# A two-layer attention and experts kernel on one Trainium2 core: the half-resolution level summed from the projected map, and two experts' first layers run inside the last image

## The chip, the cores and the metric

The kernel runs on one core of one Trainium2 chip. The core has a matrix engine (TensorE, PE in the profile; its weight loads are listed as PEld), a vector engine (VectorE, DVE), a scalar engine (ScalarE, ACT), GpSimd (POOL) and SyncE (SP), which issues most transfers. The metric is the device time of one execution in microseconds (us); the median of several runs is quoted.

## What is computed

The input is eight images of 256 channels and 32 x 32 positions, in fp32. Layer 0 is an attention with eight heads whose keys and values come from four resolutions of the projected image:

```python
kv = jnp.einsum('bchw,oc->bohw', x, kv_w)
k_map, v_map = (kv[:, :C], kv[:, C:])
def pooled(t):
    for i, r in enumerate([1, 2, 3, 6]):
        oh, ow = (round(H / r), round(W / r))       # 32, 16, 11, 5
        p = jnp.einsum('bchw,ph,qw->bcpq', t, Mh, Mw)   # averages
        p = p + _depthwise(p, dconv_w[i], dconv_b[i])   # 3 x 3
...
attn = softmax(q_g @ k * SCALE);  out_att = attn @ v
```

So there are 1024 + 256 + 121 + 25 = 1426 keys an image. Averaging and projection are both linear, so they may be done in either order. Layer 1 is a single-head attention over the 1024 tokens of an image, followed by eight experts of three 256 x 256 products each with a batch norm and a relu after the first two, weighted by a gate that is a softmax over the mean of all images:

```python
h = relu(_bn(jnp.einsum('bfd,edh->bfeh', x, W1) + b1, ...))
h = relu(_bn(jnp.einsum('bfeh,ehk->bfek', h, W2) + b2, ...))
y = jnp.einsum('bfeh,ehd->bfed', h, Wo) + bo
return jnp.einsum('bfed,fe->bfd', y, w)
```

## The kernel before

**Order of the work.** All engines' instructions are written out by a planner, the class `Flow` (lines 657 to 910), which keeps a model of each engine's clock with a price for every instruction (`cost`, line 723; GpSimd's sums are 0.15 + 0.0023 us an element, line 744). The main loop (line 1911) goes through steps: image, half of the heads, half of the queries, chunk of 128 keys. Each step issues four score products, one exponential on ACT over 2048 columns (`scores`, line 1512) and the values of the step before. Two steps' exponentials are added up by a DMA that GpSimd issues (`add`, line 1567), and `sums` (line 1574) adds the pairs on DVE. Between these, the planner resumes generator threads in the order of their rank when PE has room: a step grants 4 us of PE time to ranks below 5 and 2 us to ranks from 5 on (`PACE`, `PACE1`, lines 31 and 32, used in line 1952), and a thread may also run while PE would otherwise wait for the exponential. `finish` runs threads without that limit until something is there that the loop needs.

**Keys and values of the next image.** While image b is attended, the thread `prepare` (rank 4, line 1381) makes image b+1 ready. It normalises the image `xi`, and `pool_levels` (line 1332) makes the 16 x 16, 11 x 11 and 5 x 5 levels of it in `xl`: for each of the two channel halves, GpSimd sums neighbours in a row (`t2`, 512 elements), then neighbouring rows (`l2`, 256 elements) and multiplies by 0.25; then it makes the 11 x 11 level, and DVE the last. `maps` (line 1114) projects four maps m, two of values and two of keys, in three slices of `KEY_SLICES` (line 45): 512, 512 and 402 columns, the last being all three small levels. ACT copies each slice from PSUM into `p` and writes the centre tap of the 3 x 3 filter with its bias into `acc`. The other eight taps are DVE instructions on `p` and `acc` (`taps`, line 1245), run level after level by `convolve` (rank 7). Image 0 has its own versions, `first_maps` (line 1173) and `first_taps` (line 1259). In the narrow form (line 677) a product with 128 output rows is issued as four products of 32 rows that run side by side; the trace records two matmuls for each fp32 product.

**Layer 1 and the experts.** `layer1` (rank 6), `outputs` and `norm` (rank 5) run layer 1 of earlier images between the steps. `ended` counts the images whose normalised result `hn` is in DRAM. After the last image, attention's tiles are given up, and `experts` (line 2095) loads all weights and works on 16 tiles of 512 tokens, tile i from image i (first half) for i below 8; unit i is tile i / 8, expert i % 8. Until the gate is known it runs first and second layers ahead (`ahead`, line 2362) and puts the results into DRAM, `h2d`; after that the loop of line 2445 runs second, third and first layers in turn. The first three first layers, and all second layers before the gate, are plain: four products of 512 columns, eight records. The others take seven products of 256 columns, 14 records, with sums on DVE and GpSimd around them (`products`, line 2252).

Of the kernel before, what the change touches and what calls it, by code (L numbers as in the profile page):

```python
# [26 lines left out]
NE = 8  # L27
# [16 lines left out]
KEY_CHUNKS = [(i * P, min(P, NK - i * P)) for i in range(NKC)]  # L44
KEY_SLICES = [(0, 512), (512, 512), (1024, 402)]


# [864 lines left out]

def attention(tc, kit, f, outer, ended, nb, consts, x, t1, t2, hn, bounds, vecs, q_t, kv_t, proj_t, gqk_t, wqk, wqkv, vecs1, w1_d, w1c, gate_d, wrc, vecs2, bnvec):

# [5 lines left out]
    with ExitStack() as ctx:  # L920
# [16 lines left out]
        def load_x(b):  # L937
            xi = T(work, [P, 2, HW], "xi")
            for k in range(2):
                f.sp.dma_start(xi[:, k, :], x[b, k * P : (k + 1) * P, :])  # L940
            return xi
# [29 lines left out]
        def db(c, s):  # L971
# [5 lines left out]
            mid, vec[:, V_DW : V_DW + 72].rearrange("p (a t) -> p a t", t=9)[:, :, 4], 1.0, None, ALU.add  # L977
        )
        hi, lo = bounds
        for t in bounds:  # L980
# [129 lines left out]
        def source(xp, s0, w):  # L1110
            xi, xl = xp
            return xi[:, :, s0 : s0 + w] if s0 < HW else xl[:, :, s0 - HW : s0 - HW + w]

        def maps(xp):

            for m in (2, 3, 0, 1):
                c = m % 2
                yield until(
                    lambda: read[0] >= len(todo) - 1 and len(todo) < (3 + 2 * max(freed[0], 2) if freed[0] else 5)
                )  # L1120
                p = pmaps[len(todo) % 2]
                acc = T(work, [P, NK], "acc", bufs=3)
                for s0, w in KEY_SLICES:
                    if s0 >= HW:
                        yield until(lambda: len(done) >= len(todo) - 1)
                    src = source(xp, s0, w)
                    yield pe(src, tag="sm")
                    ps = small()
                    for k in range(2):
                        f.pe.matmul(  # L1130
                            ps[:, :w],
                            lhsT=kvw[:, k, m * P : (m + 1) * P],
                            rhs=src[:, k, :],
                            start=k == 0,
                            stop=k == 1,
                        )
                    f.act.activation(p[:, s0 : s0 + w], ps[:, :w], AF.Copy)
                    for s, n in enumerate(SIDES):
                        a, z = max(OFFS[s], s0), min(OFFS[s] + n * n, s0 + w)
                        if a < z:  # L1140
                            f.act.activation(
                                acc[:, a:z],
                                ps[:, a - s0 : z - s0],
                                AF.Identity,
                                bias=db(c, s),
                                scale=mid[:, c * 4 + s : c * 4 + s + 1],
                            )
# [7 lines left out]

        pmaps = [T(work, [P, NK], f"p{i}") for i in range(2)]
        for t in pmaps:
            f.split(t, 512, HW)
        first, large, whole, pooled, asked = {}, [], [], [], []

# [12 lines left out]
        def first_maps(xp):  # L1173
# [13 lines left out]
            for m, s0 in [(m, s0) for g in (0, 2) for s0 in (0, 512) for m in (g, g + 1)] + [(m, HW) for m in range(4)]:  # L1187
                if s0 == HW:
                    yield until(lambda: pooled)
                w = min(512, NK - s0)  # L1190
                c = m % 2
# [4 lines left out]
                for k in range(2):  # L1196
# [6 lines left out]
                    )  # L1203
                small_levels = s0 == HW and m < 2
                f.act.activation(ptail[:, m, :w] if small_levels else p[:, s0 : s0 + w], ps[:, :w], AF.Copy)
                for s, n in enumerate(SIDES):
                    a, z = max(OFFS[s], s0), min(OFFS[s] + n * n, s0 + w)
                    if a < z and (m >= 2 or s):
# [5 lines left out]
                            scale=mid[:, c * 4 + s : c * 4 + s + 1],  # L1214
                        )
                if (m, s0) == (3, 512):
                    large.append("maps")
                    f.spawn(first_keys(0), 1)
                    f.spawn(first_keys(1), 5)
# [39 lines left out]
        def first_taps():  # L1259
# [6 lines left out]
            for m in (0, 1, 2, 3):  # L1266
                p, acc = first[m]
                for s in range(1, 4):
                    yield from taps(m % 2, s, *((ptail[:, m, :], acc, HW) if m < 2 else (p, acc)))
                whole.append(m)  # L1270
            done.extend(first[m][1] for m in (2, 3, 0, 1))

        def convolve():

            for m in range(4, 4 * nb):
                yield until(lambda: len(todo) > m)
                c, p, acc = todo[m]
                for s in range(4):
                    yield from taps(c, s, p, acc)
                    read[0] += s == 0  # L1280
# [51 lines left out]
        def pool_levels(xi, xl):  # L1332
# [3 lines left out]
            def level(s):  # L1336
                n = SIDES[s]
                return xl[:, :, OFFS[s] - HW : OFFS[s] - HW + n * n].rearrange("p k (h w) -> p k h w", h=n)

            for k in range(2):  # L1340
                one, l2, l3 = img[:, k], level(1)[:, k], level(2)[:, k]

                yield pool(xi)
                t2 = T(work, [P, 32, 16], "pool")
                f.pool.tensor_tensor(t2, one[:, :, 0::2], one[:, :, 1::2], ALU.add)
                yield pool(t2)
                f.pool.tensor_tensor(l2, t2[:, 0::2, :], t2[:, 1::2, :], ALU.add)
                yield pool(t2)
                f.pool.tensor_scalar(l2, l2, 0.25, 1.0, ALU.mult, ALU.mult)

# [11 lines left out]
                f.pool.tensor_tensor(l3[:, 1:11, :], l3[:, 1:11, :], t3[:, 2::3, :], ALU.add)  # L1362
                flat = xl[:, k, OFFS[2] - HW : OFFS[3] - HW]
                f.pool.tensor_tensor(flat, flat, con[:, K_S11 : K_S11 + 121], ALU.mult)
# [8 lines left out]
            for i, (a, e) in enumerate(ends):  # L1373
                f.ve.tensor_reduce(
                    l5[:, :, i, :], t5[:, :, a:e, :].rearrange("p k h w -> p k w h"), AX.X, ALU.add
                )
            flat = xl[:, :, OFFS[3] - HW :]
            f.ve.tensor_tensor(flat, flat, con[:, None, K_S5 : K_S5 + 25].to_broadcast([P, 2, 25]), ALU.mult)
            pooled.append(True)

        def prepare(b):
# [28 lines left out]
            for k in range(2):  # L1410
# [3 lines left out]
                )  # L1414
            xl = T(work, [P, 2, NK - HW], "xl")
            if b == 0:
# [59 lines left out]
        def key_tokens(b, g):  # L1476
# [3 lines left out]
            accs = done[4 * b + 2 : 4 * b + 4] if b else [first[m][1] for m in (0, 1)]  # L1480
            kt = T(work, [P, 4, C], "kt")
            yield from by_tokens(accs, kt, 4 * g)
# [397 lines left out]
        mt = T(wp, [P, 2, C], "mt")  # L1880
        bias = T(wp, [P, 2], "mtb")
        def unit(b, c, sl, n, pairs):
            total = yield from sums(n, pairs)
# [12 lines left out]
        f.spawn(chain(mix(), weights1(), outputs()), 5)  # L1896
        f.spawn(layer1(), 6)
        f.columns = True
        order = [*range(8), NKC - 1, *range(8, NKC - 1)]
# [53 lines left out]
        f.columns = False  # L1953
        f.finish(lambda: projected[0] == nb)
        f.also.clear()
        f.finish(lambda: f.free("sx") < NEVER)
# [137 lines left out]

def experts(tc, kit, nb, t2, hn, h2d, w1c, w2_d, wo_d, bnvec, bo_d, gate_d, wrc, consts8, gtd, out, f, outer, ended, early):

# [11 lines left out]
    with ExitStack() as ctx:  # L2108
# [13 lines left out]

        w1, w2, wo = ([T(wp, [P, 2, C], f"{name}{e}") for e in range(NE)] for name in ("w1e", "w2e", "wo"))
        for e in range(NE):
            f.sp.dma_start(w1[e], w1c[:, e])
            if e == 0:
                load(0)
            f.sp.dma_start(w2[e], w2_d[:, e])
        load(1)
# [157 lines left out]

        late, stored, made = [], set(), set()

# [70 lines left out]
        s1 = {e: weights(w1[e], f"s1e{e}", wp) for e in range(NE)}  # L2360

        def ahead():
            nonlocal n1, n2

            (first if n1 < 3 else first7)(n1)
            if n1 == 0:
                ts[0] = combined(xs[0], "t1", eng=f.ve)
            n1 += 1
            f.step((PACE2, PACE2))
            if n1 > 1:  # L2370
                second(n2, True)
# [4 lines left out]
        for _ in range(NE):  # L2376
            f.step((PACE2, PACE2))
            if max(f.ready[a.name] for a in (w1[0], xs[0])) <= f.now["PE"]:
                break
        while not gated and n2 < NSTAGED:  # L2380
            ahead()
# [62 lines left out]
        weigh(0)  # L2444
        while n3 < total:
            many = n2 > n3 + 2
            if n2 < n1 - 1 or n1 == total and n2 < total:
# [13 lines left out]
def tile_conv_attn_hybrid(  # L2461
# [44 lines left out]
    last = partial(experts, tc, kit, nb, t2, hn, h2d, w1c, w2_d, wo_d, bnvec, bo_d, gate_d, wrc, consts8, gtd, out)  # L2506
    with ExitStack() as early:
        l1 = early.enter_context(tc.tile_pool(name="l1", bufs=1, side="right"))
        shared = early.enter_context(tc.tile_pool(name="psum_l1", bufs=1, space=PSUM, side="right"))
        f = Flow(tc, kit)  # L2510

        ended = [0]
        attention(
            tc, kit, f, (l1, shared), ended, nb,
            consts, x, t1, t2, hn, bounds, vecs0, q_t, kv_t, proj_t, gqk_t, wqk, wqkv, vecs1, w1_d, w1c, gate_d, wrc, vecs2, bnvec,
        )
        last(f, (l1, shared), ended, early)
    check(tc, kit, bounds, flag)
# [3 lines left out]
    with tc.If(bad > 0):  # L2522
        layer0_general(tc, kit, nb, x, t1, consts, consts8, vecs0, q_t, kv_t, proj_t, gqk_t)
        layer1_general(tc, kit, nb, t1, t2, hn, wqkv, vecs1)
        with ExitStack() as early:
            l1 = early.enter_context(tc.tile_pool(name="l1g", bufs=1, side="right"))
            shared = early.enter_context(tc.tile_pool(name="psum_l1g", bufs=1, space=PSUM, side="right"))
            last(Flow(tc, kit), (l1, shared), [nb], early)

# [110 lines left out]
```

## Time and profile before

| what | value |
|---|---|
| median of 3 runs | 3242.17 us (3239.64 to 3243.61) |
| the profiled execution's own time | 3241.38 us |
| its span, first to last instruction | 3239.2 us |
| granted PE clock, mean | 0.985 |
| idle time of PE in the span | 166.6 us |
| first and last score product | 79.9 us, 1864.8 us |
| first expert product | 1897.8 us |

The profile records one execution. A row of its groups gives the operation, what it writes and reads by the program's names, the shape, how often, the union of the times, the mean of one in ns, and the engine's idle time before it with what ended it. Nearly all instructions have line 670, the planner's wrapper, so they are told apart by their tiles: `sc` are scores, `pt` exponentials, `pv` values, `xi` and `xl` the image and its small levels, `p` and `acc` a map and its filtered form, `kvw` the projection's weights, `bank` and `y` PSUM of the experts. `pool` is a scratch tile. Some matmul records are missing from the trace.

### The profile page before, as it was taken

The page shows a single profiled execution, that of the slowest core. Times are in us where ns is not written, and L with a number is a line of the kernel's source. Part 1 is how long each engine was busy: PE and PEld are TensorE (multiplying, and loading weights), DVE is VectorE, ACT ScalarE, POOL GpSimd, SP SyncE. Part 2 cuts the span into 40 slices and gives each one's busy share as a digit, 9 for nine tenths or more (in the row PEclk, how much of TensorE's full clock was granted, in tenths as well). Part 3 has the DMA queues.
Part 4 walks back from the last instruction along what each step waited for, and adds up shares of the span by engine and source line. Part 5 has one row for each costly group of instructions (what it writes and reads, how often), then busy time and mean ns, then how long its engine had stood idle before and what let it go on. Part 6 is the DMA issues. An engine that isn't in the chain of part 4 may idle for free. (4 is left out here: it accounts for less than half of the span.)

```text
span 3239.2 us, 56567 instructions
## 1 busy us (share of the span) xinstructions
PE 3072.6 (95%) x22678; PEld 1788.4 (55%) x22678; DVE 2403.2 (74%) x4128; ACT 1690.1 (52%) x2302; POOL 1201.7 (37%) x1293
## 2 busy tenths in 40 slices
PE   8787899899999989999999999999999999999998
PEld 3322234343334333433433357777888888888887
DVE  5896888888888888788544545446878788877776
ACT  4675666666666576666655533333333333444443
POOL 2313213223232231321121220006756666777776
PEclk9898999999999999999999999999999999999999
DMA  1467665655656665655667763124344452000000
GB/s 54 93 145 160 123 140 128 145 131 126 160 122 119 158 132 106 163 120 122 145 135 144 156 213 127 59 85 169 140 153 144 148 170 72 20 24 29 20 14 21
DMA packets 117200, 375.54 MB, mean 116 GB/s; under 512 B 14512, under 2 KB 40440, under 8 KB 93696
## 3 DMA queue, kind: packets, MB, share of 16 engines
q0 software_dynamic: 28608, 179.85, 28.6%
q1 hardware_dynamic: 84960, 190.01, 17.3%
q8 instruction: 181, 2.97, 0.4%
q10 hardware_dynamic: 3360, 1.97, 0.2%
q14 instruction: 91, 0.75, 0.1%
HBM read 118.74 MB, written 87.60 MB: 64 GB/s over the span
## 5 line engine op out<-in xcount | busy, mean ns | idle before, releaser
L670 ACT ACTIVATE pt<-sc 128x2048 f32<-128x2048 f32 x352 | 660.7, 1877 | 271.2 <-PE sc L670 222.3
L670 DVE SCALAR_TENSOR_TENSOR acc<-p,vec,acc 128x961 f32<-128x961 f32 (+3 forms) x960 | 550.3, 582 | 31.6 <-ACT acc L670 6.1
L670 PE MATMUL sc<-q,kn 32*128 32x512 f32 (+1 forms) x3072 | 424.1, 653 | 98.5 <-ACT pt L670 94.8
L670 DVE TENSOR_TENSOR pt<-pt,pt 128x1024 f32<-128x1024 f32 x320 | 390.5, 1264 | 162.1 <-DMA pt<-pt 133.9
L670 PE MATMUL pv<-pt,vt 128*32 128x512 f32 x2816 | 388.8, 625 | 2.8 <-ACT vt L670 2.8
L670 ACT ACTIVATE p1c<-bank 128x256 f32<-128x256 f32 x226 | 86.4, 382 | 557.1 <-PE bank L670 545.4
L670 ACT ACTIVATE h<-h,bnvec 128x512 f32<-128x512 f32 x452 | 341.9, 805 | 61.8 <-DVE h L670 53.5
L670 POOL DMA_DIRECT2D pt<-pt x160 | 146.4, 915 | 568.4 <-ACT pt L670 435.1
L670 POOL TENSOR_TENSOR rstd<-rstd,mhalf 128x4 f32<-128x4 f32 (+2 forms) x88 | 102.7, 1168 | 614.4 <-DVE rstd L670 600.6
L670 DVE TENSOR_TENSOR h<-p1c,bank 128x512 f32<-128x512 f32 x226 | 153.9, 681 | 223.6 <-PE bank L670 216.8
L670 PEld LDWEIGHTS sc<-q,kn 32*128 32x128 f32 (+1 forms) x3072 | 114.4, 180 | 293.1 <-ACT pt L670 189.0
L670 POOL TENSOR_TENSOR tm<-h,tm 128x256 f32<-128x256 f32 x202 | 236.2, 1169 | 15.8
L670 DVE TENSOR_TENSOR h<-u,bank 128x256 f32<-128x256 f32 x452 | 230.0, 550 | 7.8
L670 PEld LDWEIGHTS pv<-pt,vt 128*32 128x32 f32 x2816 | 56.3, 109 | 279.0 <-issue 263.5
L670 PE MATMUL bank<-h,w2e 128*128 128x256 f32 (+1 forms) x620 | 204.6, 459 | 2.8 <-DVE h L670 2.0
L670 DVE TENSOR_TENSOR h<-h,gate 128x1024 f32<-128x1024 f32 x128 | 200.3, 1565 | 0.7 <-ACT h L670 0.5
L670 POOL TENSOR_TENSOR tm<-h 128x512 f32<-128x512 f32 x101 | 131.2, 1299 | 187.4 <-ACT h L670 187.4
L670 PE MATMUL sm<-p,v 128*32 128x256 f32 (+1 forms) x2424 | 199.8, 379 | 0.0
L670 PE MATMUL y<-t,s3e 128*128 128x256 f32 x768 | 187.0, 380 | 2.0 <-POOL t L670 2.0
L670 PE MATMUL bank<-t,s1e 128*128 128x256 f32 x750 | 182.5, 379 | 0.2 <-DVE h L670 0.2
L670 POOL TENSOR_TENSOR t<-h 128x512 f32<-128x512 f32 x104 | 135.4, 1302 | 109.2 <-DVE h L670 88.6
L670 PE MATMUL sm<-y,t 128*32 128x256 f32 (+1 forms) x1848 | 169.5, 382 | 5.0 <-DVE res L670 4.1
(315 smaller groups left out, 5453.2 us busy)
## 6 DMA issues: line engine op xcount, KB each, us to landing
pt<-pt POOLq DMA_DIRECT2D x160, 1024.0 KB, 7.7
h<-h SPq DMA_DIRECT2D x142, 512.0 KB
xi<-in_x_dram SPq DMA_DIRECT2D x16, 512.0 KB
t<-t SPq DMA_DIRECT2D x8, 1024.0 KB
res<-t SPq DMA_DIRECT2D x32, 256.0 KB
t<-res SPq DMA_DIRECT2D x32, 256.0 KB
hn<-res SPq DMA_DIRECT2D x32, 256.0 KB
hn<-hn SPq DMA_DIRECT2D x16, 512.0 KB
```

Source lines behind the costliest of these rows:

```text
L670: ins = fn(*args, **kwargs)
```

## The change

The second level is no longer made from the image. A new thread `halve` sums it from the projected map `p` on GpSimd, one map at a time, into `p`'s own columns 1024 to 1279, and ACT then writes its centre tap. The third slice is 146 columns, the 11 x 11 and 5 x 5 levels alone. The factor 0.25 goes into the filter's weights and the centre tap's scale. The second level's taps, and the map after the next, wait for the sum.

A new thread `experts_ahead`, of rank 8, starts when the last image's keys are ready. It loads both first layers' weights of experts 0 and 1, and first tiles of `hn`, into tiles of a new pool, `between`, that outlives attention (`xi`, `p0` and `kt` move into it), and runs these experts' first two layers in the plain form, for tiles 0 to at most 5, as long as two further units stay loaded. The experts' stage takes over the held weights and tiles, runs the units left over first, and skips what is done.

```diff
+MAP_SLICES = [(0, 512), (512, 512), (1280, 146)]
...
+        quarter = vec[:, V_DW : V_DW + 72].rearrange("p (c s t) -> p c s t", c=2, s=4)[:, :, 1]
+        f.ve.tensor_scalar(quarter, quarter, 0.25, None, ALU.mult)
+        quarter = mid.rearrange("p (c s) -> p c s", c=2)[:, :, 1]
+        f.ve.tensor_scalar(quarter, quarter, 0.25, None, ALU.mult)
...
+        def halve(p, small_p, c, acc):
+            yield pool(p[:, :HW])
+            pm = p[:, :HW].rearrange("p (h w) -> p h w", h=32)
+            t2 = T(work, [P, 32, 16], "pool")
+            f.pool.tensor_tensor(t2, pm[:, :, 0::2], pm[:, :, 1::2], ALU.add)
+            yield pool(t2)
+            l2 = small_p.rearrange("p (h w) -> p h w", h=16)
+            f.pool.tensor_tensor(l2, t2[:, 0::2, :], t2[:, 1::2, :], ALU.add)
+            yield act(small_p)
+            f.act.activation(
+                acc[:, HW : OFFS[2]], small_p, AF.Identity,
+                bias=db(c, 1), scale=mid[:, c * 4 + 1 : c * 4 + 2],
+            )
+            halved.append(acc)
...
-                for s0, w in KEY_SLICES:
+                for s0, w in MAP_SLICES:
                     if s0 >= HW:
                         yield until(lambda: len(done) >= len(todo) - 1)
+                        f.spawn(halve(p, p[:, HW : OFFS[2]], c, acc), 1)
...
                 for s in range(4):
+                    if s == 1:
+                        yield until(lambda: acc in halved)
                     yield from taps(c, s, p, acc)
...
-                t2 = T(work, [P, 32, 16], "pool")
-                f.pool.tensor_tensor(t2, one[:, :, 0::2], one[:, :, 1::2], ALU.add)
-                yield pool(t2)
-                f.pool.tensor_tensor(l2, t2[:, 0::2, :], t2[:, 1::2, :], ALU.add)
-                yield pool(t2)
-                f.pool.tensor_scalar(l2, l2, 0.25, 1.0, ALU.mult, ALU.mult)
...
+        def experts_ahead():
+            yield until(lambda: made[0] == nb and key_parts[0] == 3 * nb)
+            for e, tag in enumerate(("p0", "kt")):
+                w = held["w"][e] = T(between, [P, 2, 2, C], tag)
+                f.sp.dma_start(w[:, 0], w1c[:, e])
+                f.sp.dma_start(w[:, 1], w2_d[:, e])
+            x = T(between, [P, 2, 2, 512], "xi")
...
+            while True:
+                i = held["todo"][0]
+                h = held["x"][i // NE]
+                w = held["w"][i % NE]
+                yield pe(h, w, tag="sm")
+                if projected[0] == nb or len(held["todo"]) < 3:
+                    return
+                held["todo"].pop(0)
+                for layer in range(2):
+                    out = T(work, [P, 2, 512], "acc", bufs=3)
+                    for m in range(2):
+                        if layer or m:
+                            yield pe(h, tag="sm")
+                        ps = small()
...
+                f.sp.dma_start(h2d[i], h)
+                pre.add(i)
+                t = i // NE + 2
+                if i % NE and t < 6 and ended[0] > t:
+                    fetch(t)
...
+        aside = f.spawn(experts_ahead(), 8)
...
+        f.finish(lambda: aside[1] is None)
...
+        for i in held["todo"]:
+            xs[i // NE], usual = held["x"][i // NE], xs.get(i // NE)
+            first(i)
+            f.step((PACE2, PACE2))
+            second(i, True)
+            f.step((PACE2, PACE2))
...
+            pre.add(i)
```

In image 0, `first_maps` starts a `halve` for each map after its second slice, at rank 0, and its third slice too has 146 columns.

## Prediction

> **What bounds the kernel now.** I read the page's first part, then the busy time by stage, then who waited for whom, then the groups of instructions.
>
> ```profile
> PE 3072.6 (95%) x22678; PEld 1788.4 (55%) x22678; DVE 2403.2 (74%) x4128; ACT 1690.1 (52%) x2302; POOL 1201.7 (37%) x1293
> ```
>
> PE works 3072.6 of 3239.2 us; only 166.6 us are free. A change pays if it takes work off PE or fills those 166.6 us. The stretches (columns: stretch, length, busy time of PE, weight loads, DVE, ACT, POOL, each with its count) say where they lie:
>
> ```profile
> 83.00:537.00 454.00, 395.54 (x3558) 142.22 (x3557) 363.89 (x739) 295.06 (x357) 125.79 (x146) 0.94 0.61 133
> 537.00:1457.00 920.00, 872.60 (x8736) 345.68 (x8736) 779.88 (x1456) 608.17 (x768) 246.49 (x289) 0.99 0.62 134
> ...
> 1640.00:1867.00 227.00, 216.39 (x2424) 78.79 (x2420) 111.14 (x152) 131.34 (x124) 40.51 (x45) 0.98 0.70 146
> ...
> 2205.00:3239.20 1034.20, 1015.08 (x4660) 883.78 (x4658) 819.90 (x1150) 385.26 (x633) 695.64 (x671) 1.00 0.25 87
> ```
>
> In images 2 to 5 (second line) PE is free for 47 of 920 us, POOL for 674. From 1640 us, with the last keys made, to the last image's end (third line) PE is free for only 11 us, though DVE and ACT are half idle: layer 1 of earlier images fills PE there. The experts (last line) are PE from end to end. Of the waits in 537 to 1457 us, two matter:
>
> ```profile
> PE sc L670 <- ACT pt L670: 33.4, 34, 4.5
> ```
>
> ```profile
> DVE pt L670 <- DMA pt<-pt: 35.0, 23, 6.1
> ```
>
> PE's free time is the scores waiting for the exponential to leave their one bank group (34 times, 33.4 us). DVE has 140 us without work, and waits in order for the rows that a DMA adds. Both stand near full, PE nearer.
>
> **Part one, the second level.** (1) *PE.* The third slice of each projection falls from 402 to 146 columns.
>
> ```profile
> L670 PE MATMUL sm<-xi,kvw x560: 592/592/1062, 17.7 to 1491.0; 128*32 128x512 f32 x173, 128*128 128x512 f32 x14
> L670 PE MATMUL sm<-xl,kvw x212: 497/501/606, 51.9 to 1429.9; 128*32 128x402 f32 x88, 128*128 128x402 f32 x18
> ```
>
> 110 columns fewer make 592 into 501 ns (medians): 0.83 ns a column, 0.212 us for 256. A map has four such passes (two halves of the input, two records each; in the narrow form four strips run side by side, so a pass costs the same): 0.85 us. Four maps of eight images: 32 x 0.85 = 27 us less PE work.
>
> (2) *ACT.* The copy of the slice falls from 402 columns (506 ns) towards 146; 512 columns take 595, so 0.81 ns a column and 0.21 us a map, 6.6 us in all. The level's Identity stays (560 ns for 256 columns from PSUM; from SBUF the nearest row, the scaling of the key tokens, takes 592): 32 x 0.03 = 1 us back. ACT works 66% of the images, so I count nothing; the range has the 6 us.
>
> (3) *POOL.* Per image the change removes, for each of two halves, a row sum, a column sum and the factor 0.25, and adds four pairs of sums. The rows of 537 to 1457 us:
>
> ```profile
> L670 POOL TENSOR_TENSOR pool<-xi 128x512 f32<-128x512 f32 x8 | 13.0, 1624 | 6.0 <-DVE xi L670 6.0
> L670 POOL TENSOR_TENSOR xl<-pool 128x256 f32<-128x256 f32 x8 | 7.7, 968 | 0.4
> L670 POOL TENSOR_SCALAR xl<-xl 128x256 f32<-128x256 f32 x8 | 5.4, 677 | 0.3
> L670 POOL DMA_DIRECT2D pt<-pt x80 | 73.7, 921 | 252.0 <-ACT pt L670 195.5 <-DVE acc L670 24.2 <-PE sm L670 19.8
> ```
>
> Added 4 x (1.62 + 0.97) = 10.4 us, removed 2 x (1.62 + 0.97 + 0.68) = 6.5: 3.9 us more an image, 31 in all, on an engine that is 73% free. That cover is not used up. The two factors folded into the taps' weights at the start are two DVE instructions of about 0.17 us (row `mid`), before the first tap.
>
> (4) *DVE.* Its instructions are the same. The second level's taps now wait for the sum. Eight first-level taps (about 1.22 us each, 9.8 us) run ahead of them; the sum needs 2.6 us, perhaps an exponential of 1.88 on ACT, and 0.56. So the wait is hidden, with some 5 us to spare. POOL's rows, though, are stretched: the same sums take 1.04 and 0.73 us where DVE leaves them alone (21.8 and 22.9 us into the span). A collision can cost DVE as much as POOL. Bounds: 0, and 8 x 3.9 = 31 us of DVE time. DVE's 140 us without work in 920 absorb most; I take 1. In image 0 nothing moves: the third slices start at 51.9 us, behind the first keys' products on PE, and POOL has been done with the levels since 29 us.
>
> The Trainium skill (SBUF — State Buffer, Who interferes with whom) says that a DVE instruction with two SBUF inputs and a GpSimd instruction that reads SBUF block one another for a whole instruction; taps and sums are such a pair. By that rule every added microsecond of POOL would come off DVE, the 31 us above. The stretched rows agree in kind; nothing in the trace shows DVE paying in full.
>
> (5) *The added wait on ACT.* The Identity of the second level waits on ACT for POOL, and behind it queues the next exponential, for which PE waits. The planner issues it when it believes the sum done: by its prices (lines 744 and 740) the pair takes 1.33 + 0.74 = 2.07 us; the rows have 2.59. So each of 28 waits (images 1 to 7) can stall up to 0.52 us: 0 to 15 us. If POOL stands behind a DMA that waits for its exponential (195.5 / 80 = 2.4 us, then 0.92), 3.3 us each, 93 in all. A gain is impossible here. I take 3, near the lower end, since the planner prices those DMAs too.
>
> **Part two, the thread.** (6) *How much it runs.* Its rank is 8, behind layer 1 (5 and 6), and these share 2 us of PE credit a step (lines 31 and 32). From 1640 to 1867 us there are 54 steps (the exponentials of that stretch), 108 us of credit. Layer 1 used 216.4 - 63.2 (scores) - 62.8 (values) - 5.2 (sums) - 7.6 (projection) = 78 us. Left are 30. A unit (two layers, 3.44 us each: eight 512-column records of `bank<-h,w2e`) takes 6.9, so 4 or 5 units; 10 is the most, when layer 1 is late.
>
> (7) *What that is worth.* The same layers cost seven products in the experts, by the chain of work:
>
> ```profile
> 2770.31 6.04 PE bank L670 x28
> ```
>
> 28 records are two layers in 6.04 us, 3.02 each. So a moved unit costs 6.88 us and gives back 6.04. Since PE is nearly full in the last image, moving is no gain by itself: 5 units lose 4 us, and the four units held over at the end, run in the plain form too, about 1 more. Against this the thread can fill the 11 free us of that stretch; I take 5.
>
> (8) *The change of stage.* The held tiles let PE start without loads:
>
> ```profile
> 1886.63 8.80 PE L670 MATMUL sm<-y,t 128*128 128x256 f32 x40
> 1897.81 7.11 PE L670 MATMUL bank<-hn,w1e 128*128 128x512 f32 x16 [2.39 <-DMA hn<-hn]
> ```
>
> The 2.39 us go. SP issues four weight loads fewer there and some ten more transfers of 512 KB in the last image, whose DMA share is 0.70; nothing waits behind them but loads two tiles ahead. The relus (0.78 us, four a unit) lie on an ACT that is 58% busy. More results lie staged before the third layers begin, so the stretch with two thirds a turn is longer: PE is 99% busy there as after it; 1 us.
>
> **The sum**, against the profiled execution's 3241.4 us (span 3239.2 and 2.2 around it; the median of the three runs is 3242.2). PE's 27 us do not all become time, since some steps end with the exponential whatever PE does: PE's free share there is 5%, DVE's 15%; I take four fifths, 22. Then -22 + 1 + 3 + 4 + 1 - 5 - 2.4 + 1 = -19, so 3222, and 3223 by the median. I say 3222.
>
> The skill also holds (Perfetto Trace Analysis, Identifying the Most-Contended Engine) that matmul occupancy is a bad measure and weight-load occupancy a good one. By that, PE in the images is at 38% (345.7 of 920), and the 27 us would be worth nothing. The trace's 0.83 ns a column and the scores' waits of only 33 us in 920 are why I go by occupancy.
>
> **Rivals.** *A: DVE sets the pace of the images.* Then PE's saving is only more waiting, and the time is about 3241 - 2.4 - 3 = 3236. For it: 780 of 920 us busy plus 114 of in-order waits. Against it: layer 1 always has work for PE to do earlier. It would show as PE's idle time in the images growing by some 20 us. *B: POOL holds ACT (slower).* The Identity stands in ACT's queue while POOL waits for the DMA before the sum. If 14 of the 28 meet it, 14 x 3.3 = 46 us, against 3 counted: 3241 - 19 + 43 = 3265. It decides above 0.8 us a map (22 / 28). Against it: POOL is 73% free, and the planner knows that queue. *C: more gain.* ACT's 6 us shorten steps, all 27 us count, the thread fills all free PE time: 3241 - 27 - 6 - 11 - 2 + 6 = 3201. *D: the thread gets no credit and does nothing but hold two tiles:* 3241 - 22 + 1 + 3 - 2.4 = 3221, the forecast again; counted with it.
>
> **How the numbers follow.** Forecast with D 0.58 (3210 to 3235), A 0.17, B 0.13, C 0.12. A measurement of this kernel can tell 0.2% (6.5 us) from no change. Faster takes forecast, C and a quarter of A: 0.74; the same has most of A: 0.14; slower has B and a little: 0.12. The range runs from C, less 3 us, to the forecast with step 5 at its 15 us and half of step 4's 31 us of collisions, less the 4 counted there (12 + 14): 3198 to 3248.
>
> **What would show it.** Step 1: the third slice's rows with 146 columns at about 0.28 us, PE's total about 22 us lower (27 less the plain form's 5). Step 3: 56 row sums in the images, 1.0 to 1.7 us. Step 5: ACT idle before `acc` with POOL as its releaser, under 15 us. Step 6: 4 to 10 units stored before 1890 us. Step 8: no gap between the last projection and the first expert. I am wrong if PE's idle total grows by over 15 us, or if ACT waits for POOL over 0.8 us a map.

## The result, and the profile after

The changed kernel takes 3258.45 us (median of five runs, 3253.80 to 3261.13), the kernel before 3242.17 (five runs, 3236.77 to 3244.22): a ratio of 1.0053, 95% interval 1.0041 to 1.0065. It is 16 us slower where 19 us less were forecast, and outside the range of 3198 to 3248. The profiled execution has a span of 3259.2 us, 20 more than before.

The page's first part, after:

```profile
PE 3056.5 (94%) x22330; PEld 1789.3 (55%) x22330; DVE 2406.7 (74%) x4117; ACT 1682.6 (52%) x2301; POOL 1240.7 (38%) x1327
```

PE works 16.1 us less (3072.6 before), yet its idle time rose from 166.6 to 202.7 us: 36 us of new waiting ate the saving and 20 more. VectorE's total hardly moved, GpSimd's rose by 39.0 us. Images 2 to 5 (to set beside the prediction's second line) and the last image alone, each from its first exponential; columns as before:

```profile
525.80:1475.60 949.80, 872.16 (x8502) 350.97 (x8505) 767.04 (x1421) 598.04 (x753) 275.00 (x311) 0.97 0.60 131
...
1705.00:1899.90 194.90, 192.28 (x2192) 71.33 (x2188) 93.10 (x133) 115.83 (x113) 36.67 (x39) 1.00 0.68 142
```

The last image alone in the kernel before:

```profile
1680.00:1867.00 187.00, 178.84 (x2052) 66.65 (x2052) 93.35 (x135) 108.89 (x104) 34.68 (x39) 0.99 0.71 147
```

Images 2 to 5 took 920 us and now take 950; PE's work in them is the same 872 us, its clock 0.97 against 0.99, and its free time 78 us against 47. VectorE is *less* busy there, 767 against 780. The last image leaves PE 2.6 us free, where it was 8.2: the thread fills it. The last exponential ends at 1899.9 us, where before it ended at 1867.4 (32.5 later); what follows takes 1359.3 us, 12.5 less than 1371.8.

The two groups that the change aimed at (count, then duration least / median / most in ns, first and last start), and the sums on GpSimd:

```profile
L671 PE MATMUL sm<-xl,kvw x284: 285/288/392, 52.4 to 1550.1; 128*32 128x146 f32 x128, 128*128 128x146 f32 x14
...
L671 POOL TENSOR_TENSOR pool<-p x30: 1028/1040/2003, 36.8 to 1550.7; 128x512 f32<-128x512 f32 x30
L671 POOL TENSOR_TENSOR p<-pool x30: 728/753/1786, 38.0 to 1551.8; 128x256 f32<-128x256 f32 x30
```

A pass of the third slice fell from 0.501 to 0.288 us, as step 1 said. Now the waits between 83 and 1690 us (engine, what waited, for whom; us in total, times, longest), first before, then after:

```profile
PE sc L670 <- ACT pt L670: 86.8, 67, 6.5
...
ACT pt L670 <- DMA pt<-pt: 30.6, 11, 6.0
```

```profile
POOL pool L671 <- ACT p L671: 160.8, 25, 11.2
PE sc L671 <- ACT pt L671: 119.1, 93, 6.2
ACT pt L671 <- DMA pt<-pt: 71.7, 22, 7.3
...
ACT acc L671 <- POOL p L671: 11.9, 8, 3.4
```

PE waits 32 us more for exponentials, and these 41 us more for their buffers, whose rows an adding DMA has still to read. The added wait (last line) is 11.9 us. The first line looked like the culprit: GpSimd stands 161 us in front of its sums until ScalarE has copied the map, with the adding DMAs queued behind it.

### The profile page after: what moved, and what is told of

It is laid out like the page before. It is cut to its first block, busy times and chain, and to the rows that moved or that the text cites. A ratio compares the mean times of both kernels' runs of the same rounds, so it can differ in the third digit from the quotient of the medians.

```text
span 3259.2 us, 55911 instructions
## 1 busy us (share of the span) xinstructions
PE 3056.5 (94%) x22330; PEld 1789.3 (55%) x22330; DVE 2406.7 (74%) x4117; ACT 1682.6 (52%) x2301; POOL 1240.7 (38%) x1327
## 4 chain that ended last, share of the span: by engine, by line
PE 49%; DVE 6%; DMA 3%; issue 2%; ACT 2%; POOL 1%; SPq 0%; DVEq 0%; POOLq 0%; ACTq 0%
PE bank L671 20%; PE y L671 10%; PE sm L671 9%; PE sx L671 4%; PE sc L671 3%; PE pv L671 3%; DVE h L671 2%; DMA pt<-pt 2%; ACT pt L671 1%; DVE acc L671 1%; DVE u L671 1%; DVE c L671 1%; DVE pt L671 1%; DVE t L671 0%; DMA t<-res 0%
## 5 line engine op out<-in xcount | busy, mean ns | idle before, releaser
L671 DVE SCALAR_TENSOR_TENSOR acc<-p,vec,acc 128x961 f32<-128x961 f32 (+3 forms) x960 | 562.2, 594 | 35.1 <-ACT acc L671 9.4
L671 POOL TENSOR_TENSOR t<-h,t 128x256 f32<-128x256 f32 x214 | 169.5, 792 | 16.8
L671 DVE TENSOR_TENSOR u<-h,bank 128x512 f32<-128x512 f32 x225 | 154.7, 688 | 24.7 <-PE bank L671 1.4
L671 PEld LDWEIGHTS y<-t,s3e 128*128 128x128 f32 x768 | 145.7, 190 | 24.0 <-POOL t L671 2.5
```

The source lines that it names most:

```text
L671: ins = fn(*args, **kwargs)
```

## The experiments

Three theories stood at first. **Stops**: those 161 us delay the adding DMAs. **Collisions**: sums and taps slow each other down. **Order**: the planner reacts to the new instructions with another order of all the others, and that order is worse. Each time stands beside the kernel before on the same chip, whose median was 3238.6 to 3240.4 us there; ratios are to it, with the 95% interval, and differences in us are what these ratios lack of or have above 1, times 3240.

**The two parts alone.** Part one without the thread:

```diff
-        aside = f.spawn(experts_ahead(), 8)
+        aside = [None, None, 8]
```

> Part one alone: the second level summed from the projected map, no thread for the experts. My theory is that the sums do the harm: image starts as after up to image 6 (1475 us), attention ends near 1885 to 1895 us where before has 1867, and the experts' stage is as long as before (1372 us), so 3255 to 3265 us, PE's idle total 190 us or more. The rival that blames the thread wants PE's saving to appear here: 3220 to 3230 us.

Measured 3279.49 us, 1.0126 (1.0109 to 1.0143): slower than the whole change. The last exponential ends at 1897.5 us, and PE is idle for 210.8 us. So part one alone does the harm. By the ratios it lies 24 us above the whole change; the profiles show 11 of them (spans of 3269.9 and 3259.2), mostly because the execution profiled here was 8 us shorter than this run's median and that of the whole change 3 us longer than its own.

Part two without part one (the second level from the image again, `KEY_SLICES` in the maps, no `halve`):

> Part two alone: the second level summed from the image as before, the thread kept. My theory is that the thread costs the last image about what the experts give back: image starts as before up to image 6, the last image 7 to 20 us longer, the experts' stage 10 to 20 us shorter, 3235 to 3247 us. The rival that blames the thread: 3255 us or more.

Measured 3238.79 us, 0.9992 (0.9982 to 1.0002): -2.6 us, no change that can be told. Its last image and its experts:

```profile
1690.30:1885.00 194.70, 192.19 (x2168) 71.82 (x2164) 93.33 (x135) 115.58 (x113) 35.07 (x39) 1.00 0.71 149
1885.00:3237.70 1352.70, 1327.89 (x5900) 1107.57 (x5892) 967.54 (x1418) 496.85 (x828) 740.57 (x749) 0.99 0.26 88
```

The attention ends 17.6 us later (1885.0 against 1867.4), and the rest is 19.1 us shorter: a net of -1.5.

**Stops against collisions, in the order of after.** Two runs keep every instruction at its place and change what the sums do in images 1 to 7. In the first, the first sum reads a constant tile and is accounted as before:

```diff
-            f.pool.tensor_tensor(t2, pm[:, :, 0::2], pm[:, :, 1::2], ALU.add)
+            if len(halved) < 4:
+                f.pool.tensor_tensor(t2, pm[:, :, 0::2], pm[:, :, 1::2], ALU.add)
+            else:
...
+                ins = nc.gpsimd.tensor_tensor(d, o0, o1, ALU.add)
+                f.note("POOL", "tensor_tensor", ins, (t2, pm[:, :, 0::2], pm[:, :, 1::2], ALU.add), {})
```

> The changed kernel with the same instructions in the same order on every engine, but in images 1 to 7 the first sum on GpSimd reads a constant tile that was ready from the start, in place of the projected map, so the second level holds sums of constants; GpSimd no longer stands still for ScalarE's copy of the map with DMAs queued behind it. Theory one (those stops delay the adding DMAs, and with them the exponentials and the scores): the 161 us in which GpSimd waits for p go, the exponentials' wait for the added rows falls from 67 us towards 31, and the time falls by 15 to 25 us, to 3235 to 3243. Theory two (VectorE and the chain of preparation are slower through collisions) and theory three (the order itself is worse): within 5 us of the changed kernel's 3258.

Measured 3260.66 us, 1.0062 (1.0048 to 1.0077): nothing gained. The stops are gone from its list of waits, and the same two waits stand as they were:

```profile
PE sc L671 <- ACT pt L671: 120.3, 88, 6.2
ACT pt L671 <- DMA pt<-pt: 73.8, 24, 7.1
```

ScalarE's wait for the sums is down to 3.4 us too (11.9 in the changed kernel). So the theory of the stops falls. In the second run the sums are short:

```diff
-            f.pool.tensor_tensor(t2, pm[:, :, 0::2], pm[:, :, 1::2], ALU.add)
+                ins = nc.gpsimd.tensor_tensor(t2[:, 0, :8], pm[:, 31, 0:16:2], pm[:, 31, 1:17:2], ALU.add)
...
-            f.pool.tensor_tensor(l2, t2[:, 0::2, :], t2[:, 1::2, :], ALU.add)
+                ins = nc.gpsimd.tensor_tensor(l2[:, 0, :8], t2[:, 0, :8], t2[:, 0, :8], ALU.add)
```

> The changed kernel in the same order, but in images 1 to 7 the two sums on GpSimd run over 8 columns only, which leaves most of the second level at what it was before; the first still reads the last row of the projected map, so GpSimd's stops for the copy stay. Theory two (the sums' time and their collisions with the taps make the keys late): 10 us or more below the changed kernel, the taps' busy time back from 562 to about 550 us. Theory one (the stops): the gain is no more than the sums' own 1.1 us each where they are waited for, 5 us at most. Theory three (the order): within 5 us too.

Measured 3245.59 us, 1.0022 (1.0010 to 1.0034): 13 us below the run without stops, 10 below the changed kernel.

```profile
PE 3049.7 (94%) x22330; PEld 1788.2 (55%) x22330; DVE 2388.3 (74%) x4117; ACT 1685.1 (52%) x2301; POOL 1206.2 (37%) x1327
```

Against the changed kernel VectorE loses 18.4 us of work with the same instructions, GpSimd 34.5. Collisions are real, though how much of the 10 to 13 us is theirs and how much is the sums' own time on GpSimd, this run does not separate. Even without the sums' work this order is 7 us slower than before, though PE is busy for 23 us less (3049.7 against 3072.6).

**Old and new work in the old and the new order.** A small addition to the planner allows this: `ghost` accounts for an instruction that isn't issued, `aside` issues one that isn't accounted for.

```diff
+    def ghost(self, engine, op, *args):
+        last, self.last = self.last, {}
+        self.note(engine, op, Ghost, args, {})
+        self.last = last
+
+    def aside(self, engine, op, *args, **kwargs):
+        names = ("now", "ready", "read", "writer", "reader", "port")
+        state = [dict(v) if isinstance(v, dict) else v for v in (getattr(self, n) for n in names)]
+        ins = getattr(engine.eng, op)(*args, **kwargs)
+        self.note(engine.name, op, ins, args, kwargs)
+        for n, v in zip(names, state):
+            setattr(self, n, v)
```

First only the shorter third slice (steps 1 and 2), in the order of before:

```diff
-                    f.act.activation(p[:, s0 : s0 + w], ps[:, :w], AF.Copy)
+                    ins = nc.scalar.activation(p[:, s0 + cut : s0 + w], ps[:, cut:w], AF.Copy)
+                    f.note("ACT", "activation", ins, (p[:, s0 : s0 + w], ps[:, :w], AF.Copy), {})
```

and the products likewise, `cut` being 256 in the third slice.

> The kernel before, with every engine's instructions in the order of before, but in images 1 to 7 the third slice of each map is projected and copied in 146 columns in place of 402; the second level of these maps is then left at zero (its centre tap reads that), and the sums from the image stay though nothing uses them. It measures steps 1 and 2 of the prediction alone, for 28 of 32 maps: 28 x 0.85 = 24 us of PE and 28 x 0.21 = 6 us of ScalarE. If PE's saving is worth what the prediction says (four fifths), 19 us less than before, 3223 us. If the steps end with something else (VectorE, the exponential, the added rows), 5 us less at most.

Measured 3227.78 us, 0.9961 (0.9948 to 0.9974), so 12.6 us less than before. Of PE's 24 us about half became time, not four fifths, even with ScalarE's 6 us beside them. Then the whole of part one for images 1 to 7, in the order of before (`sum2` is a `ghost` there):

```diff
+                f.aside(f.pool, "tensor_tensor", rows, pm[:, :, :, 0::2], pm[:, :, :, 1::2], ALU.add)
+                f.aside(f.pool, "tensor_tensor", l2, rows[:, :, 0::2, :], rows[:, :, 1::2, :], ALU.add)
                 todo.append((c, p, acc))
...
-                f.pool.tensor_tensor(t2, one[:, :, 0::2], one[:, :, 1::2], ALU.add)
+                sum2("tensor_tensor", t2, one[:, :, 0::2], one[:, :, 1::2], ALU.add)
```

> Part one of the change, whole and with the reference's result, for images 1 to 7, but set into the order of before: the planner's accounts are those of before, the sums from the projected map stand on GpSimd behind the map's third slice, the second level's centre tap on ScalarE behind the fourth first-level tap, and the three operations on the image are gone. If the order that the planner writes after the change is what costs the time, this is faster than before by what the prediction gave, 3220 to 3228 us. If the sums themselves, where they stand now, cost it (waits for ScalarE's copy, collisions with the taps), it is slower than before: 3250 us or more, with the taps' busy time up by 12 us or more.

Measured 3235.43 us, 0.9986 (0.9973 to 0.9998): 4.5 us less than before. It lies between the two expectations, nearer to that of the order. The page's first parts of these two runs:

```profile
PE 3049.2 (95%) x22678; PEld 1784.5 (55%) x22678; DVE 2402.4 (75%) x4128; ACT 1682.4 (52%) x2302; POOL 1203.0 (37%) x1295
```

```profile
PE 3058.4 (95%) x22678; PEld 1786.9 (55%) x22678; DVE 2420.6 (75%) x4130; ACT 1680.7 (52%) x2302; POOL 1223.7 (38%) x1307
```

Adding the sums and dropping those on the image costs GpSimd 20.7 us and VectorE 18.2, and takes 8 us of the 12.6 back. The mirror, again for images 1 to 7: the work of before, in the order that the planner writes for part one.

```diff
+            if ghost:
...
+                f.ghost("POOL", "tensor_tensor", t2, pm[:, :, 0::2], pm[:, :, 1::2])
...
+                    f.aside(f.pool, "tensor_tensor", t2, one[:, :, 0::2], one[:, :, 1::2], ALU.add)
+                    f.aside(f.pool, "tensor_tensor", l2, t2[:, 0::2, :], t2[:, 1::2, :], ALU.add)
+                    f.aside(f.pool, "tensor_scalar", l2, l2, 0.25, 1.0, ALU.mult, ALU.mult)
```

> The mirror of the run that set part one into the old order: here images 1 to 7 do the work of before (second level summed from the image with its factor, third slice of 402 columns, centre tap from PSUM), set into the order that the planner writes for part one alone; the result is the reference's. If the order is the cause, this is as slow as part one alone or slower by the work that came back: 3275 to 3295 us. If the new work is the cause, it is near before: 3235 to 3250 us.

Measured 3291.89 us, 1.0156 (1.0143 to 1.0169), with the work of before.

| us against before, by the ratio | order of before | order written for part one |
|---|---|---|
| work of before | 0 | +51 |
| work of part one | -5 | +41 |

Down a column the work changes, and the kernel gets 5 or 10 us faster. Along a row the order changes, and it gets 51 or 45 us slower. The traces show that the order was held: PE's groups of products and SyncE's transfers follow one another alike in both kernels of a column (but for two of 2949 groups of products in the old order), while the exchanged sums stand where they were put by hand. The two waits go with the order, not with the work. Old work in the new order, then new work in the old order (83 to 1690 us):

```profile
PE sc L676 <- ACT pt L676: 115.5, 81, 8.1
ACT pt L676 <- DMA pt<-pt: 81.0, 22, 8.4
```

```profile
PE sc L675 <- ACT pt L675: 85.9, 66, 6.7
...
ACT pt L675 <- DMA pt<-pt: 26.0, 9, 6.0
```

The whole change in the order that the planner writes for the thread alone (the same edits as in the run of part one in the old order, images 1 to 7, on top of the thread):

> The whole change in the order of before: part one set into the order that the planner writes for the thread alone. If the two effects add, -4.5 us (part one in the old order) and -1.6 us (thread alone) give 3233 us; if the thread's extra load meets the sums, 3240 us or more.

Measured 3232.46 us, 0.9981 (0.9971 to 0.9991), so -6 us (-9 to -3). Part one in the old order (-4.5) and the thread alone (-2.6) make -7: the parts add up once the order is held.

**How far one order lies from another.** If the order counts for 45 to 51 us, a constant that changes no work should move the time as well. `MARGIN` says how long ahead of its need an operand must be believed ready:

```diff
-MARGIN = 1.5
+MARGIN = 1.6
```

> The kernel before with one constant of the planner moved (MARGIN 1.5 to 1.6, how far ahead of need an operand has to be believed ready before a thread gets PE): the same work in another order. If the order alone moves the time by as much as the change did, it is 10 us or more away from before's 3241, in either direction; if the order hardly matters, within 5 us.

> Part one alone with the same constant moved (MARGIN 1.6): the work of the run with the sums alone (3279 us) in another order. If the order is what costs the time there, 10 us or more away from it, in either direction; if the sums cost it wherever they stand, within 5 us of it.

> The kernel before with MARGIN 1.4: the same work in a third order. If the order of before is a lucky one among its neighbours, 15 us or more above before, as with 1.6 (3270 us); if 1.6 was unlucky, within 10 us.

> Part one alone with MARGIN 1.4: the work of the runs at 3279 and 3259 us in a third order. If the loss is of the order alone, the three lie as far apart as those of the kernel before, and this one may fall below 3250 us; if part one brings a loss of its own in any order that the planner writes, it is again at 3255 us or more.

> The kernel before with MARGIN 1.45: a fourth order of the same work. If the order of before is a lucky draw, 3250 us or more like the two others (3258 and 3270 us); if orders near 1.5 are good as a rule, within 10 us of 3240.

> Part one alone with MARGIN 1.45: a fourth order. If it is all scatter, anywhere between 3225 and 3280 us, and the mean of the four near that of before's four; if part one brings bad orders as a rule and 3231 us at 1.4 was the exception, 3260 us or more.

> The whole change with MARGIN 1.4, the value at which part one alone took 3231 us. If the order decides, the whole change is faster than before as well: 3225 to 3235 us. If the change itself loses the 18 us, 3250 us or more.

> The whole change with MARGIN 1.6, at which part one alone took 3259 us and before 3270 us. If the order decides: within 10 us of part one alone there, less what the thread gives, 3240 to 3260 us. If the change itself loses 18 us: about 3288 us.

> The whole change with MARGIN 1.45. If the change is worth about its predicted 19 us on the average and the order adds a scatter of 10 to 25 us, 3220 to 3245 us; if 1.4 and 1.6 were exceptions and the change as a rule loses, 3255 us or more.

| MARGIN | before, us | ratio | part one, us | ratio | whole change, us | ratio |
|---|---|---|---|---|---|---|
| 1.4 | 3258.05 | 1.0057 (1.0044-1.0069) | 3230.73 | 0.9969 (0.9957-0.9982) | 3222.80 | 0.9950 (0.9937-0.9964) |
| 1.45 | 3261.08 | 1.0065 (1.0050-1.0081) | 3233.13 | 0.9985 (0.9976-0.9994) | 3227.69 | 0.9962 (0.9949-0.9975) |
| 1.5 | 3240 | 1 | 3279.49 | 1.0126 (1.0109-1.0143) | 3258.45 | 1.0053 (1.0041-1.0065) |
| 1.6 | 3269.87 | 1.0089 (1.0070-1.0108) | 3258.84 | 1.0054 (1.0037-1.0071) | 3243.41 | 1.0010 (1.0001-1.0019) |
| mean | 3257 | | 3251 | | 3238 | |

All ratios are to the kernel before at 1.5. 1.6 alone sent before up by 29 us and part one down by 23, and 1.4 and 1.45 sent part one and the whole change below before, where the theory of a lasting loss had expected 3250 us and more. The order of before is the best of its four, that of part one at 1.5 the worst of its four, and so is the whole change's. The differences whole change less before are -35, -33, +18 and -26 us, with a mean of -19; their spread (standard deviation 25 us, so some 13 us on the mean of four) makes the agreement with the forecast's -19 worth little, though in three of four orders the change is faster. The loss lies in different places: in the run of before at 1.6 the last exponential ends at 1865.7 us, as early as before, and the experts take 1397 us instead of 1372; in part one at 1.5 the attention takes it all.

The whole change at 1.4 is faster than both kernels, 3222.80 us. Its page and waits (83 to 1690 us):

```profile
PE 3042.0 (95%) x22720; PEld 1785.3 (55%) x22720; DVE 2408.7 (75%) x4120; ACT 1683.0 (52%) x2304; POOL 1264.3 (39%) x1345
```

```profile
POOL pool L671 <- ACT p L671: 112.4, 20, 12.8
PE sc L671 <- ACT pt L671: 92.5, 81, 6.0
...
ACT pt L671 <- DMA pt<-pt: 48.3, 16, 6.1
```

PE's work is 30.6 us below before, its idle time 175.2 us (166.6 before, 202.7 in the change at 1.5). GpSimd still stands 112 us in front of its sums, at no visible cost.

## Why the prediction was wrong, step by step

1. **Third slice on PE: right in size, wrong in worth.** 0.213 us a pass came out. Taking in each stretch of 10 us from 80 to 1900 us PE's busy time, times what the granted clock lacks of 1.00, PE lost 29.9 us to a reduced clock before and 42.1 after, so its work at full clock fell from 3042.7 to 3014.4 us, 28 us, where the forecast was 27 less up to 5 for the plain form. But "I take four fifths" fails: in an unchanged order 12.6 us of 24 (with ScalarE's 6) became time. Nor were they worth nothing, as weight-load occupancy would have had it.
2. **ScalarE:** 7.5 us less work in total. Not measured apart from step 1.
3. **"That cover is not used up"** holds for GpSimd's own time: 39.0 us more for a forecast 31, and even 161 us of standing in front of the sums cost nothing.
4. **The sums: mis-sized.** Steps 4 and 5 counted 1 us for collisions and 3 for ScalarE's wait; the sums cost 8 us in the old order, where no wait of ScalarE for them shows, and 10 to 13 in the new one. VectorE pays 18.2 us for 20.7 us of GpSimd's. The sentence "nothing in the trace shows DVE paying in full" was true of the trace and no reason for the low end.
5. **The added wait:** 11.9 us in 8 waits, the longest 3.4, within the bound of 15. Without the stops in front of the sums, and with 3.4 us of that wait, the time stayed. Rival B, which ended on the side that came, is not the cause.
6. **The thread** began 3 units, not 4 or 5, and the stores of two were issued before 1890 us.
7. and 8. **Their balance fits:** +4 +1 -5 -2.4 +1 = -1.4 against -2.6 measured for the thread alone (-5.8 to +0.6). No run separates the terms, and with 3 units in place of 5 some of the agreement may be luck. PE's free time in the last image fell from 8.2 to 2.5 us there, near the 5 of step 7.

**The step that failed is "The sum".** It adds the steps to the profiled execution's time as if all else stayed where it was. Held in the order of the thread alone, they give -6 us: a third of the forecast, since step 1 was worth 9 us less than counted and steps 4 and 5 cost 4 us more. The rest of the way, from -6 to +17, is the order that the planner wrote afresh: it prices each instruction and picks the next thread by what it believes ready, so 32 shorter slices and 32 pairs of sums moved the others too. The prediction put that term at nothing, without a reason, and it stands in no rival. Its scatter, 30 to 49 us among four orders of the same work, is wider than the effect, and the starting point was the best of its four orders. The one sentence that bore on it, that PE's idle total must not grow by over 15 us, was the right alarm (it grew by 36), but behind it I had put VectorE: rival A's sign came, not its cause, since VectorE's share of images 2 to 5 fell.

What stays open is why one order makes exponentials wait 72 to 81 us for added rows and another 26 to 31. How late GpSimd issues those adding DMAs, behind the exponential that they need, does not tell the orders apart: the sum over 160 of them is 309 us before, 382 after, 340 in the run without stops (no faster), and 388 in the fastest kernel of all. Nor do they take longer to land: 7.7 us in the median before and after, 8.0 in the fastest. No run isolates a feature of the order itself.

## What to carry to other kernels

Where a planner writes the order from prices, a change in any price is a change of the whole order: move a constant that does no work first, and take that scatter as the least width of the forecast. Compare work in a held order (accounts kept, instructions exchanged) before believing or dropping a change; here it separated -6 us of work from +23 of order. A kernel that was measured best among its neighbours starts with an advantage that an edit may lose by the new order alone, so judge an edit over several orders of both versions.

## What the runs showed of the hardware

**Idle stretches on PE cost clock as well.** The granted clock in rows of 10 us, of before:

```profile
380.00:390.00 10.00, 8.80 (x76) 2.19 (x72) 9.93 (x9) 5.64 (x3) 5.38 (x5) 1.00 0.78 152
390.00:400.00 10.00, 6.45 (x44) 1.79 (x44) 9.58 (x18) 4.94 (x6) 1.09 (x4) 0.70 0.75 152
400.00:410.00 10.00, 10.00 (x140) 4.27 (x136) 9.12 (x18) 5.37 (x5) 0.87 (x1) 0.95 0.34 68
410.00:420.00 10.00, 10.00 (x100) 4.60 (x92) 5.33 (x15) 6.80 (x12) 0.80 (x1) 1.00 0.33 67
```

PE is 3.5 us idle from 390 us on, the clock falls to 0.70 and is back at 1.00 after 410. Over all the profiles of this case (80 to 1850 us), 1818 such rows had less than 1 us of idle time in themselves and the row before taken together: the clock was 1.00 in every one. With 3 to 5 us its mean was 0.914 (429 rows), with more 0.862 (294). So the 36 us of new waiting came with 12 us of slower products. The total of idle time does not set this loss: part one at 1.4 is idle for 22 us more than before and loses 26.8 us, less than before's 29.9. The Trainium skill (TensorE: Matmul & The Clock Gate, HAM oscillation) warns of gaps above about 3.4 us; the rows agree in kind, though 64 of the 803 rows with 1 to 3 us of idle time are below 1.00 too.

**GpSimd's sums and VectorE's taps lengthen each other.** In part one in the old order a second-level tap of 225 elements takes 0.45 us alone and 0.84 on the average with a two-tensor instruction of GpSimd beside it (17 of 112, 9 of them with one of the new sums). VectorE's work grows by 18.2 us with 20.7 us added on GpSimd. The Trainium skill (SBUF — State Buffer, Who interferes with whom) says that a VectorE instruction with two SBUF inputs contends with a GpSimd instruction that reads SBUF, and calls the lock on the ports that they share exclusive; the whole instruction, of which the prediction speaks, it names only for VectorE's two-port modes. The measured 0.88 us for each microsecond is near to what that would give, while in the new order it was 18.4 of 34.5.
